# Decoder layers on one core: in the last attention, the queries' maxima reach all partitions by two DMAs and are put in order by ScalarE, and the exponentials run six steps behind the scores

## The chip, the cores and the metric

The kernel runs on one core of a Trainium2 chip. The core has TensorE (PE in the profile; PEld is its weight load), VectorE (DVE), ScalarE (ACT), GpSimd (POOL) and SyncE (SP), which here only issues DMAs. The metric is device time of one execution in microseconds, the median of several runs. Before the change it was 2773.41 us (three runs, 2769.01 to 2780.34).

## The reference

Four decoder layers of width 128 over a batch of 4 with 256 tokens each. Each layer has a self-attention, a cross-attention to a context of 1601 rows of width 96, and a feed-forward block, each followed by a residual and a layer norm. The change touches the last cross-attention only, which has 16 heads of 64:

```python
def _L3_xattn_ref(x, context, Wq, Wk, Wv, Wo, bo):
    HEADS, DIM_HEAD = 16, 64
    b, n, _ = x.shape                                   # 4, 256
    h, d = (HEADS, DIM_HEAD)
    scale = d ** (-0.5)
    q = (x @ Wq).reshape(b, n, h, d).transpose(0, 2, 1, 3)
    k = (context @ Wk).reshape(b, -1, h, d).transpose(0, 2, 1, 3)
    v = (context @ Wv).reshape(b, -1, h, d).transpose(0, 2, 1, 3)
    sim = jnp.einsum('bhid,bhjd->bhij', q, k) * scale
    attn = jax.nn.softmax(sim, axis=-1)
    out = jnp.einsum('bhij,bhjd->bhid', attn, v)
    out = out.transpose(0, 2, 1, 3).reshape(b, n, h * d)
    return out @ Wo + bo

x = _layernorm(x + _L3_xattn_ref(x, ctx_768, ...), axis=-1)
x = _layernorm(x + _L3_ffn_ref(x, ...), axis=-1)
```

The softmax subtracts, for each query and head, the maximum over all 1601 keys.

## The kernel before

All data is float32 but for a few masks and the last feed-forward. The program is a row of stages (`STAGES`, L2125); the last is `l3_xattn` (L1865). On PE, VectorE and ScalarE the order of its instructions is the order in which the code issues them (`manual_schedule`, L2060). Each engine works through its own list and stops at the first instruction whose input or buffer isn't ready. SP's list holds, in this stage, only the loads at its start and the four stores of the output.

A **unit** is one batch element and one pair of heads (L1875): 4 x 8 = 32 units. Head h of the pair lies in partitions 64h to 64h + 63 of the Q and K tiles. A unit has four **steps**: the keys in three groups of 512 and one of 65 (`parts`, L1888, splits a step into tiles of up to two chunks of 128 keys). I call a step of 512 keys full and one of 65 short. The loop at L2061 makes one pass for each step g, and in a pass does, for several steps at once:

- `queries` (L1894), once in a unit: Q of both heads, evicted by VectorE.
- `projections(g + 1, gb)` (L1902): K of the next step and V of step gb = g - LAG, into one PSUM tile, both evicted by ScalarE (L1931).
- `scores(g)` (L1933): keys in partitions, queries along the row. ScalarE copies the PSUM tile to an SBUF tile `St` (L1943).
- `running(g - 1)` (L1945): VectorE takes the elementwise maximum of the `St` tiles, so that after four steps there is one tile of 128 partitions x 2 heads x 256 queries.
- `maxima` (L1959), once in a unit: PE transposes this tile by matmuls with the identity, and VectorE reduces over the 128 keys (L1969). The result `mq` holds, in partition t, the four maxima of query t (2 heads x 2 halves of the queries).
- `spread` (L1971), once in a unit, one pass later: PE multiplies each column of `mq`, broadcast to 64 columns, with the identity, so that the maxima of all queries stand as a row in every partition. ScalarE copies this from PSUM to `Mb` (L1981).
- `shifted(gb)` (L1983): VectorE subtracts `Mb` from the `St` tiles of step gb. `weights(gb)` (L1991): ScalarE takes the exponentials in place.
- `sums(gb - 1)` (L1996): PE multiplies the exponentials with V into an accumulator that lives over the unit's four steps, and with ones for the row sums. After the fourth step ScalarE copies the row sums to `rows` (L2026).
- `ended` (L2029), issued one pass later by `advance(later)` (L2075): PE adds up the row sums, VectorE takes the reciprocal (L2035) and the product (L2038). After a batch element's eight units the output projection follows, and one pass at a time its layer norm and the last feed-forward (`l3_ffn`, L2087). `later` begins with what two batch elements have left over from the stage before, a feed-forward with GELU (L1796) among it.

PSUM has three large tiles for scores and projections (`big`) and two banks for all the rest (`misc`, named `one` in the profile); the accumulator holds one of the two banks for most of a unit. The lag is five steps and there are 12 `St` tiles. `kept` (L1883) is a part of a weight slot that is free by then; the running maximum and the leftovers live in it. Nearly all matmuls are recorded under L399, the helper `mm`.

## Time and profile before

| | |
|---|---|
| median of three runs | 2773.41 us |
| the profiled execution | 2769.6 us |
| its span | 2767.8 us, granted clock 0.98 |
| PE busy | 2620.8 us, 95% |
| VectorE busy | 1747.2 us, 63% |
| ScalarE busy | 1526.2 us, 55% |
| chain that ended last | PE 88%, DVE 6%, ACT 3% |
| the last attention | about 1896 us to the end |

The profile is one execution. The span runs from its first to its last instruction; the time of the execution is 1.8 us longer. Busy times are per engine, and engines overlap. Of a group of instructions the profile gives the line, the engine, the operation, the tile written and the tiles read with their shapes, the count, the busy time and the mean in nanoseconds; after it stands the idle time just before these instructions and what ended it. The chain that ended last follows the work back from the last instruction, at each step to what released it; it is given as start, length, engine, tile, line and count. `issue` is time in which an engine waited for nothing that the profile shows.

### The profile page before, as it was taken

The page shows a single profiled execution, that of the slowest core. Times are in us where ns is not written, and L with a number is a line of the kernel's source. Part 1 is how long each engine was busy: PE and PEld are TensorE (multiplying, and loading weights), DVE is VectorE, ACT ScalarE, POOL GpSimd, SP SyncE. Part 2 cuts the span into 40 slices and gives each one's busy share as a digit, 9 for nine tenths or more (in the row PEclk, how much of TensorE's full clock was granted, in tenths as well). Part 3 has the DMA queues.
Part 4 walks back from the last instruction along what each step waited for, and adds up shares of the span by engine and source line. Part 5 has one row for each costly group of instructions (what it writes and reads, how often), then busy time and mean ns, then how long its engine had stood idle before and what let it go on. Part 6 is the DMA issues. An engine that isn't in the chain of part 4 may idle for free.

```text
span 2767.8 us, 63295 instructions
## 1 busy us (share of the span) xinstructions
PE 2620.8 (95%) x26619; PEld 1708.1 (62%) x26619; DVE 1747.2 (63%) x3802; ACT 1526.2 (55%) x2931; POOL 180.2 (7%) x199
## 2 busy tenths in 40 slices
PE   6999999988879999999899999999999999999997
PEld 4555555555555555555797777776566666666665
DVE  5666666465457665655355666666677677677675
ACT  2455555635534555555554555556666576576573
POOL 2000100120020000000001011111000000000000
PEclk8999999989999999999999999999999999999999
DMA  3000000000120000000002010000000000000000
GB/s 111 2 1 1 2 1 1 1 21 15 27 88 17 2 1 1 1 2 1 1 1 87 20 25 13 13 12 3 1 1 2 4 2 1 3 2 2 3 2 3
DMA packets 14684, 34.57 MB, mean 12 GB/s; under 512 B 4025, under 2 KB 7229, under 8 KB 13505
## 3 DMA queue, kind: packets, MB, share of 16 engines
q1 hardware_dynamic: 14400, 30.53, 4.0%
q8 instruction: 210, 3.44, 0.5%
q14 instruction: 74, 0.60, 0.1%
HBM read 23.67 MB, written 0.52 MB: 9 GB/s over the span
## 4 chain that ended last, share of the span: by engine, by line
PE 88%; DVE 6%; ACT 3%; issue 2%; POOL 1%; DMA 0%; POOLq 0%; ACTq 0%; DVEq 0%
PE one L399 63%; PE big L399 13%; PE acc L399 8%; DVE M L909 1%; PE one L835 1%; PE one L544 1%; PE one L472 1%; DVE St L1987 1%; PE one L1324 1%; DVE mpad L697 1%; ACT E L731 0%; DVE w L1953 0%; DVE rec L2035 0%; POOL rn L1257 0%; ACT w L1314 0%
## 5 line engine op out<-in xcount | busy, mean ns | idle before, releaser
L909 DVE TENSOR_REDUCE M<-one 128x1 f32<-128x458 f32 (+3 forms) x1024 | 528.2, 567 | 290.8 <-PE one L399 289.8
L932 ACT ACTIVATE E<-one 128x512 f32<-128x512 f32 (+1 forms) x896 | 457.7, 563 | 420.8 <-PE one L399 420.7
L399 PE MATMUL one<-Q,K 32*128 32x256 f32 (+1 forms) x3328 | 531.8, 402 | 1.5 <-DVE M L909 1.5
L399 PE MATMUL one<-K,Q 32*128 32x458 f32 (+3 forms) x2048 | 459.2, 541 | 1.6 <-DVE M L909 1.6
L399 PEld LDWEIGHTS one<-Q,K 32*128 32x128 f32 (+1 forms) x3328 | 310.6, 180 | 62.3 <-DVE M L909 35.5
L1943 ACT COPY St<-big 128x1024 f32<-128x1024 f32 (+1 forms) x224 | 204.3, 959 | 160.0 <-PE big L399 160.0
L399 PEld LDWEIGHTS one<-K,Q 32*128 32x128 f32 x2048 | 171.2, 185 | 143.8 <-issue 79.3
L1987 DVE TENSOR_TENSOR St<-St,Mb 128x1024 f32<-128x1024 f32 (+1 forms) x224 | 245.2, 1141 | 1.8 <-ACT Mb L1981 1.8
L399 PE MATMUL acc<-E,V 128*32 128x256 f32 (+1 forms) x3328 | 233.2, 387 | 7.1 <-ACT E L932 7.1
L1994 ACT ACTIVATE St<-St 128x1024 f32<-128x1024 f32 (+1 forms) x224 | 215.1, 1014 | 25.4 <-DVE St L1987 25.3
L731 ACT ACTIVATE E<-one 128x384 f32<-128x384 f32 (+1 forms) x352 | 154.3, 525 | 115.0 <-PE one L399 114.8
L399 PE MATMUL big<-Q,K 64*128 64x256 f32 (+1 forms) x1664 | 214.4, 393 | 0.0
L399 PE MATMUL one<-St,V 128*64 128x256 f32 (+1 forms) x1664 | 205.7, 384 | 0.4
L492 POOL TENSOR_TENSOR ln_r<-ln_ve,half 128x2 f32<-128x2 f32 x92 | 71.0, 772 | 2070.0 <-DVE ln_ve L490 2015.8
L1953 DVE TENSOR_TENSOR w<-w,St 128x1024 f32<-128x1024 f32 (+1 forms) x160 | 178.5, 1116 | 34.8 <-ACT St L1943 27.6
L399 PE MATMUL one<-xT,w 128*128 128x256 f32 (+1 forms) x664 | 170.9, 398 | 18.8 <-DVE Q L1127 8.3
L692 DVE TENSOR_REDUCE Ms<-one 128x3 f32<-128x384 f32 x256 | 130.1, 550 | 89.0 <-PE one L399 87.8
L399 PEld LDWEIGHTS big<-Q,K 64*128 64x128 f32 (+1 forms) x1664 | 147.7, 183 | 57.5 <-issue 40.2
L399 PEld LDWEIGHTS acc<-E,V 128*32 128x32 f32 (+1 forms) x3328 | 87.3, 109 | 125.0 <-issue 70.0
L399 PEld LDWEIGHTS one<-St,V 128*64 128x64 f32 (+1 forms) x1664 | 114.3, 137 | 63.4 <-issue 15.9
L399 PEld LDWEIGHTS big<-w,ctx 96*64 96x64 f32 x1664 | 96.8, 137 | 54.0 <-issue 53.9
L399 PEld LDWEIGHTS one<-xT,w 128*128 128x128 f32 (+1 forms) x664 | 97.1, 181 | 50.2 <-issue 15.6
(308 smaller groups left out, 3743.7 us busy)
## 6 DMA issues: line engine op xcount, KB each, us to landing
QK<-qk SPq DMA_DIRECT2D x256, 16.0 KB
w<-in_p SPq DMA_DIRECT2D x12, 274.0 KB
rows<-in_ctx_rows SPq DMA_DIRECT2D x4, 630.5 KB
ctx<-in_ctx SPq DMA_DIRECT2D x4, 600.4 KB
w<-in_down SPq DMA_DIRECT2D x1, 2112.0 KB
w<-in_up SPq DMA_DIRECT2D x1, 1632.0 KB
w<-in_gp SPq DMA_DIRECT2D x1, 1632.0 KB
w<-in_p SPq DMA_DIRECT2D x4, 384.0 KB
```

Source lines behind the costliest of these rows:

```text
L399: self.nc.tensor.matmul(out, lhsT, rhs, start=start, stop=stop)
L472: self.nc.tensor.transpose(ps[:, n * P : (n + 1) * P], x[:, n, :], self.ident)
L492: nc.gpsimd.tensor_tensor(rstd, ve, self.half[:, :NB], ALU.pow)
L544: self.nc.tensor.transpose(ps[:rows, n * P : (n + 1) * P], m4[:, n, :rows], self.ident)
L692: nc.vector.reduce_max(out=m[:, j, :], in_=ps[:, : 3 * P].rearrange("p (s c) -> p s c", c=P), axis=AX.X,)
L731: nc.scalar.activation(es[t, j], ps[:, :w], AF.Exp, scale=scale)
L909: nc.vector.reduce_max(out=ms[i][:, n, j, part : part + 1], in_=ps[:, at : at + hi - lo], axis=AX.X)
L932: nc.scalar.activation(e[:kp, :w], ps[:kp, :w], AF.Exp, scale=scale)
L1943: nc.scalar.copy(st[:kp, :, :nc_, :], ps[:kp, :, :nc_, :])
L1953: nc.vector.tensor_max(to, to, sts[u, k][:kp, :, :nc_, :])
L1987: nc.vector.tensor_sub(e, e, top[u][:kp].unsqueeze(2).broadcast_to([kp, 2, nc_, T]))
L1994: nc.scalar.activation(e, e, AF.Exp, scale=HD**-0.5)
```

## The change

Spread's matmuls and its copy are replaced. The result `mq` of a unit's maxima (128 partitions x 4) is stored by a DMA into a DRAM tile `mrow`, and a second DMA reads it back, one row of 512 values to every partition, into `home`. In this row the four maxima of a query stand side by side. `order` has ScalarE copy it to `ordered`, where the queries of one head and half are contiguous. `home` and `ordered` lie in 1024 columns that are added to the tiles of two weight packs (`SPARE`); the slots of those packs have room for these columns, since larger packs use them earlier.

The DMAs are issued in the pass of `maxima`, right behind it; `order` comes two passes later, just before the first `shifted` of the unit, with the lag now six. `shifted` moves from ahead of `queries` and `projections` to behind them. `running` moves in one of four passes from the end of the pass to its beginning. There are 14 `St` tiles, and they are laid out chunk first, then head.

```diff
+SPARE = {"p4": 1024, "p3_3": 1024}
...
+        self.dram_pool = pool("dram", 2, space=bass.MemoryType.DRAM)
...
-        t = self.tile(f"w{SLOT[name]}", [P, src.shape[1]], pool=self.wpool)
+        t = self.tile(f"w{SLOT[name]}", [P, src.shape[1] + SPARE.get(name, 0)], pool=self.wpool)
...
-        HD, LAG = 64, 5
+        HD, LAG = 64, 6
...
+        o = self.dram["p3_3"].shape[1]
+        ordered = self.packs["p3_3"][:, o : o + 1024].rearrange("p (i j t) -> p i j t", i=2, t=P)
+        home = self.packs["p4"][:, 3 * NH * HD :].rearrange("p (i c) -> p i c", i=2)
...
-                st = self.tile("St", [P, 2, 2, T], bufs=12)
+                st = self.tile("St", [P, 2, 2, T], bufs=14)
                 sts[u, k] = st
-                nc.scalar.copy(st[:kp, :, :nc_, :], ps[:kp, :, :nc_, :])
+                nc.scalar.copy(
+                    st[:kp, :nc_, :, :].rearrange("p c h t -> p h c t"), ps[:kp, :, :nc_, :]
+                )
...
         def spread(u):
-            ps, m = self.misc(), mx.pop(u)
-            for j in range(2 * NB):
-                for d in halves:
-                    self.mm(
-                        ps[d, j * P : (j + 1) * P],
-                        m[:, j : j + 1].broadcast_to([P, HD]), self.ident,
-                    )
-            top[u] = self.tile("Mb", [P, 2, T], bufs=2)
-            nc.scalar.copy(top[u].rearrange("p h t -> p (h t)"), ps)
+            row = self.tile("mrow", [P, 2 * NB], bufs=2, pool=self.dram_pool)
+            nc.sync.dma_start(row, mx.pop(u))
+            top[u] = home[:, u % 2]
+            nc.sync.dma_start(
+                top[u], row.rearrange("t j -> (t j)").unsqueeze(0).broadcast_to([P, 2 * T])
+            )
+
+        def order(u):
+            nc.scalar.copy(ordered[:, u % 2], top.pop(u).rearrange("p (t j) -> p j t", j=2 * NB))
 
         def shifted(g):
             u = g // 4
+            m = ordered[:, u % 2].unsqueeze(1)
             for k, nc_, kp in parts(g):
-                e = sts[u, k][:kp, :, :nc_, :]
-                nc.vector.tensor_sub(
-                    e, e, top[u][:kp].unsqueeze(2).broadcast_to([kp, 2, nc_, T])
-                )
+                e = sts[u, k][:kp, :nc_].rearrange("p c h (n t) -> p c (h n) t", n=NB)
+                nc.vector.tensor_sub(e, e, m[:kp].broadcast_to([kp, nc_, 2 * NB, P]))
...
                 gb = g - LAG
-                if g % 4 < 2 and 0 <= g - 1 < steps:
+                if g % 4 < 3 and 0 <= g - 1 < steps:
                     running(g - 1)
-                if g % 4 == 1 and 4 < g <= steps + 1:
-                    spread(g // 4 - 1)
-                if 0 <= gb < steps:
-                    shifted(gb)
                 if 0 <= g + 1 < steps and (g + 1) % 4 == 0:
                     queries((g + 1) // 4)
                 if g + 1 < steps or gb < steps:
                     projections(g + 1, gb)
+                if 0 <= gb < steps:
+                    if gb % 4 == 0:
+                        order(gb // 4)
+                    shifted(gb)
                 if 0 <= gb < steps:
                     weights(gb)
                 self.advance(later)
...
                 if g % 4 == 0 and 4 <= g <= steps:
                     maxima(g // 4 - 1)
-                if g % 4 > 1 and 0 <= g - 1 < steps:
+                    spread(g // 4 - 1)
+                if g % 4 == 3 and 0 <= g - 1 < steps:
                     running(g - 1)
```

Where the diff is left out, `running`, `weights` and `sums` index the `St` tiles in the new layout.

More of the change, by code (lines that the diff above doesn't have):

```diff
@@ L1948, in running @@
                 if k == 1:
-                    mx[u] = kept[:, :4].rearrange("p (h c) t -> p h c t", h=2)
+                    mx[u] = kept[:, :4].rearrange("p (c h) t -> p c h t", h=2)
                     nc.vector.tensor_max(mx[u], sts[u, 0], sts[u, 1])
                 elif k:
-                    to = mx[u][:kp, :, :nc_, :]
-                    nc.vector.tensor_max(to, to, sts[u, k][:kp, :, :nc_, :])
+                    to = mx[u][:kp, :nc_]
+                    nc.vector.tensor_max(to, to, sts[u, k][:kp, :nc_])
             if g % 4 == 3:
@@ L1956, in running @@
                 mx[u] = self.tile("mx", [P, 2, T], bufs=2)
-                nc.vector.tensor_max(mx[u], m[:, :, 0, :], m[:, :, 1, :])
+                nc.vector.tensor_max(mx[u], m[:, 0], m[:, 1])
         def maxima(u):
@@ L1971, in spread @@
         def spread(u):
-            ps, m = self.misc(), mx.pop(u)
-            for j in range(2 * NB):
-                for d in halves:
-                    self.mm(
-                        ps[d, j * P : (j + 1) * P],
-                        m[:, j : j + 1].broadcast_to([P, HD]), self.ident,
-                    )
-            top[u] = self.tile("Mb", [P, 2, T], bufs=2)
-            nc.scalar.copy(top[u].rearrange("p h t -> p (h t)"), ps)
+            row = self.tile("mrow", [P, 2 * NB], bufs=2, pool=self.dram_pool)
[6 more added lines that the diff above has]
+            nc.scalar.copy(ordered[:, u % 2], top.pop(u).rearrange("p (t j) -> p j t", j=2 * NB))
         def shifted(g):
             u = g // 4
+            m = ordered[:, u % 2].unsqueeze(1)
             for k, nc_, kp in parts(g):
-                e = sts[u, k][:kp, :, :nc_, :]
-                nc.vector.tensor_sub(
-                    e, e, top[u][:kp].unsqueeze(2).broadcast_to([kp, 2, nc_, T])
-                )
+                e = sts[u, k][:kp, :nc_].rearrange("p c h (n t) -> p c (h n) t", n=NB)
+                nc.vector.tensor_sub(e, e, m[:kp].broadcast_to([kp, nc_, 2 * NB, P]))
         def weights(g):
             for k, nc_, kp in parts(g):
-                e = sts[g // 4, k][:kp, :, :nc_, :]
+                e = sts[g // 4, k][:kp, :nc_]
                 nc.scalar.activation(e, e, AF.Exp, scale=HD**-0.5)
@@ L2007, in sums @@
                             self.mm(
-                                acc[d, :T], vs[g][:, i - g % 4 * 4, d], e[:, h, c, :],
+                                acc[d, :T], vs[g][:, i - g % 4 * 4, d], e[:, c, h, :],
                                 start=i == 0, stop=False,
@@ L2016, in sums @@
                         self.mm(
-                            acc[d, T:], self.w("c", "ones", kp)[:, :SW], e[:, h, c, :],
+                            acc[d, T:], self.w("c", "ones", kp)[:, :SW], e[:, c, h, :],
                             start=False, stop=False,
@@ L2021, in sums @@
                     for h, d in enumerate(halves):
-                        self.mm(acc[d, :T], vs[g][:kp, 0, d], e[:, h, 0, :], start=False)
+                        self.mm(acc[d, :T], vs[g][:kp, 0, d], e[:, 0, h, :], start=False)
             vs.pop(g)
```

## The prediction

> **What bounds the kernel now.** I read first the page's busy times:

> ```profile
> PE 2620.8 (95%) x26619; PEld 1708.1 (62%) x26619; DVE 1747.2 (63%) x3802; ACT 1526.2 (55%) x2931; POOL 180.2 (7%) x199
> ```

> The changed stage is the last third of the span (about 1896 to 2767 us). The busy times of one stretch of it, one unit in the middle (columns: PE, PEld, DVE, ACT and POOL busy, granted clock, DMA share, GB/s):

> ```profile
> 2283.10:2307.68 24.58, 24.58 (x266) 15.43 (x264) 17.93 (x19) 16.86 (x24) 0.00 (x0) 1.00 0.01 1
> ```

> PE has no gap in 24.58 us, VectorE 6.7 us of gaps, ScalarE 7.7. So a PE instruction removed here is worth its whole length until another engine makes PE wait. The chain that ended last, over the same unit:

> ```profile
> 2283.10 3.75 PE one L399 x48
> 2286.85 1.93 PE big L399 x16
> 2288.78 1.02 PE one L399 x16
> 2289.80 1.73 PE big L399 x20
> 2291.53 1.14 PE one L399 x8
> 2292.67 3.07 PE big L399 x36
> 2295.74 3.16 PE one L399 x36
> 2298.90 1.93 PE big L399 x16
> 2300.83 0.58 PE one L399 x4
> 2301.41 1.73 PE big L399 x20
> 2303.15 2.73 PE one L399 x32
> 2305.88 1.81 PE big L399 x12
> ```

> Read as code: 3.75 is a full `sums` (2.73) and `maxima` (1.02); 1.93 `scores`; the second 1.02 is `spread`; 1.73 a full K and a full V projection; 1.14 the short `sums`; 3.07 is scores, short K and full V (so 1.14 for these two); 3.16 is `ended` (0.44) and sums; 0.58 `queries`; 1.81 is short scores (0.6), full K (0.86), short V (0.35).

> The instructions that the change touches, in groups over six units:

> ```profile
> L1987 DVE TENSOR_TENSOR St<-St,Mb 128x1024 f32<-128x1024 f32 x36 | 41.9, 1218 | 0.0
> L1994 ACT ACTIVATE St<-St 128x1024 f32<-128x1024 f32 x36 | 36.6, 1080 | 0.0
> ...
> L399 PE MATMUL one<-c,mq 128*64 128x128 f32 x96 | 6.6, 279 | 0.0
> ...
> L1981 ACT COPY Mb<-one 128x512 f32<-128x512 f32 x6 | 3.5, 586 | 0.0
> ```

> For the DMAs, an earlier stage's timeline has a small transfer on an empty queue, and the end has a store to DRAM:

> ```profile
> 1498.32 8.06 SPq L1850 DMA_DIRECT2D QK<-qk  x12
> ...
> 1501.03 0.40 PEld L399 LDWEIGHTS one<-QK 32*128 32x128 f32 x4 [2.31 <-DMA QK<-qk]
> ...
> 2765.16 0.37 SPq L2122 DMA_DIRECT2D out<-x  x1
> ```

> So 2.71 us from issue to use, and at most 2.64 for the store (the span ends at 2767.8).

> **Removed.** Spread's 16 PE instructions, 1.02 us in each of 32 units, all on the path. Its ScalarE copy (0.59) goes too; ScalarE isn't the bound.

> **Added: two DMAs a unit on SP's queue.** SP issues nothing else in this stage but four output stores, which wait for their block; a store issued just ahead costs the pair its issue (0.37), inside the spare time below. First, 16 bytes from each partition to DRAM: nearest row the store, 2.6. Second, 2 KB to each of 128 partitions: 2.7 as in the row, plus its packets. The page gives 14400 packets and 4.0% of 16 engines' span, so 0.123 us each; 8 an engine make 1.0. It can't start before the first has landed: 2.6 + 3.6 = 6.2 us. Bounds: 4.3 (twice 2.17, the shortest, QK<-w from 555.95 to 558.12) and 12.1 (twice 6.05, the longest DMA piece in the chain, four issues one behind another). I take 6.2, as nothing else is on the queue. [...]

> What hides them: the wait sits in ScalarE's queue at `order`, in the second step after maxima. From the end of maxima's matmuls PE does scores 1.93, K and V 1.21, sums 2.73, scores 1.93, K and V 1.14: 8.94. Call that end t0. ScalarE's turn comes at t0 + 0.7 (two copies). The reduction ends 1.1 after its matmuls (0.691 by its row, L1969, and up to 0.4 behind the shift of the same step). The pair may take 8.94 + 0.7 - 1.1 = 8.5; 2.3 are spare. Behind a late `order` stand, on ScalarE, this step's exponentials, the row-sum copy and the score evictions; PE waits for them.

> **Added: ScalarE's order**, 512 elements read 16 bytes apart: nearest row the 0.586 copy it replaces (contiguous, from PSUM). Bounds 0.4 (the 256-element copies, 0.373) and 2.3 (four times 0.586, as the read spans four times the bytes; no row excludes it). I take 0.59. [...]

> **Moved: shift after order, inside the same step.** At the step of t0 VectorE first does two running maxima (1.22 each), from t0 - 0.8, when the first eviction is there, to t0 + 1.65. ScalarE's order, from 0.7 to 1.3, hides behind them. Then two shifts (to 2.87 and 4.05), exponentials at 1.03 to 1.08 behind them (to 5.12), rows' copy (0.37, overlapping a little): 5.4. PE reaches `ended`, which reads rows, at t0 + 1.14 + 1.93 + 0.58 + 1.73 = 5.38. Before, the rows were there at 2294.87 and PE came at 2295.57, 0.7 spare; now none. I allow 0.1 a unit, +3 us; bounds 0 and 0.3 (+10). Every other pair keeps its order with room: maxima's input is done 0.9 before PE asks. The query copy now stands ahead of the shift; PE's wait for it at the three batch ends (0.48 each) should go: -1.4.

> **Same length:** the score copies, maxima, shifts and exponentials in the new layout move the same elements in runs of 128 or more; 224 of each, so 0.05 us apiece either way would stay in the 6 us of gaps. If those were gone, 4 x 224 x 0.05 = 45 us.

> **One step more behind.** Head: one more step without sums, PE work only moved. The first `order` has a shorter budget (6.5 us less 0.8), so +1. The GELU chain at 1996.6 to 2001.8, where PE waited 4.2 us for ScalarE, now falls on a short step (exponential 0.63 for 2.02): -1.4. Tail: after the last maxima PE has one full sums and a short V more left (3.1), which earlier lay ahead. Chain: reduction 0.75, pair 6.2, order 0.6, shift 1.2, two exponentials 2.1, rows 0.4, ended 0.44, then 2.73 + 0.97 + 2.73 + 0.35 + 2.73 + 1.14: 22.3. Before, 2724.24 to 2743.5: 19.3. 22.3 - 3.1 - 19.3 = 0, with the last unit's spread already inside; each us more of the pair costs one more here.

> **Sum:** 31 x 1.02 = -31.6; +3; -1.4; +1; -1.4; 0: -30.4. The profiled execution (2769.6, span 2767.8) would become 2739. It lies 3.8 under the median of the runs, 2773.4, so the median becomes 2743.

> **Rivals.**
> *The pair is late (slower).* Beyond 8.5 us, ScalarE's order starts late; 0.35 more hides behind the running maxima; from 8.85 each us costs PE one us in each unit, 32 in all. At 9.8 us (4.9 each) the gain is gone; at 12.1, 32 x 3.25 - 30 = +74: 2847. For it: 128 sixteen-byte packets to DRAM and a load at once behind them, which no row shows. Against: three rows of 2.2 to 2.7.
> *Order is slow.* Above 0.95 us it delays the shifts. At twice the row: 0.2 x 32 = 7 lost, 2750; at 2.3: 1.4 x 32 = 44, 2787.
> *The wait moves to rows (part of the gain).* At 0.3 a unit: 2750. For it: the zero margin above.
> *The change doesn't do what it says.* The DMA lands in spare columns of the tile that holds Wq, Wk, Wv. If projections waited for it as for the whole tile, PE would stand some 5 us a unit: +130, 2900. Against: the QK row, where matmuls of one tile's first 32 partitions start while its other DMAs are still out.

> **How the numbers follow.** Near the forecast (2734 to 2749) 0.58; part of the gain, by rows or order (2749 to 2759) 0.18; gain eaten to within 0.5% (about 14 us, what a measurement can tell here) 0.08; pair late, slower 0.09; order slow, slower 0.03; whole-tile waits and the rest 0.04. Low end 2734: no 0.1 allowance, no head cost, and 5 for a better head; high end 2766: reaches into the third case, leaving about 0.17 above. Faster 0.77, same 0.08, slower 0.15.

> **What would show it.** Right: a unit of 23.6 us with PE full; no `one<-c,mq` matmuls; ScalarE's order some 0.6 us without a wait on a DMA of any length in the middle of the stage; exponentials starting later after K and V. Wrong: PE or PEld waiting for ScalarE rows (L2026's successor) or the shift in each unit; ScalarE waiting for a DMA before order; order's mean over 1 us; PE waiting for a DMA at the projections. The forecast fails if the pair takes 9 us or more, or order more than 1 us.

## The result, and the profile after

The changed kernel takes 2781.51 us (median of 20 runs, 2773.02 to 2794.39), the kernel before beside it 2773.55 us (20 runs, 2765.99 to 2782.38). The ratio is 1.0031, 95% interval 1.0021 to 1.0041: a little slower, where 2743 us, 1.1% faster, was forecast. The profiled execution of the changed kernel spans 2779.3 us.

TensorE's code is now recorded under L402, the score copies under L1950, the order under L1992, the shift under L1999, the exponentials under L2004, the copy of the row sums under L2036.

A clock for the stage that needs no interpretation is the start of each unit's reduction to `mq` (L1969 before, L1978 after). From the timelines:

| us | before | after | forecast |
|---|---|---|---|
| one unit in the middle | 24.59 | 24.18 | 23.67 |
| the two intervals from the second batch end (reduction 16 to 18) | 59.95 | 63.27 | 57.6 |
| head: reduction 0 to 5 | 140.0 | 142.6 | 131.9 |
| all 31 intervals | 809.4 | 811.9 | 775.9 |
| tail: reduction 31 to the end of the span | 43.5 | 48.5 | 46.5 |
| reduction 0 to the end | 853.0 | 860.3 | 822.4 |

The last column is the forecast's own terms: 0.92 off each unit (1.02 removed, 0.1 allowed), 0.47 off each batch end, +1 - 1.4 at the head, and 3.1 us of sums and projections moved from the head (the longer lag) to the tail, where the chain was to be 3.0 longer (22.3 against 19.3). The stage is 7.3 us longer, close to the 8.0 between the medians. Everything ahead of the stage runs the same instructions in the same order in both kernels, so what the two spans differ by ahead of reduction 0 (4.1 us) is mostly how these two executions fell: in the kernels below, reduction 0 starts anywhere from 1911.8 to 1928.5 us.

So TensorE lost its 16 instructions in a unit, and gained much less. The busy times of one unit in the middle of the changed kernel (columns as before: the length, then PE, PEld, DVE, ACT and POOL busy, granted clock, DMA share, GB/s):

```profile
2229.00:2253.17 24.17, 23.93 (x250) 14.58 (x248) 18.03 (x18) 17.69 (x25) 0.00 (x0) 1.00 0.04 12
```

PE, full before, has a gap. The chain that ended last shows what ended it, in the same unit:

```profile
2228.41 0.82 ACT St L1950
2229.23 0.09 issue
2229.32 1.02 ACT St L1950
...
2230.41 0.21 ACT K L1938
2230.63 0.49 ACT V L1938
2231.11 1.03 ACT w L1992
2232.15 0.02 issue
2232.17 2.37 DVE St L1999 x2
...
2234.67 0.86 issue
2235.53 0.36 ACT rows L2036
2235.89 0.04 issue
2235.94 3.38 PE one L402 x36
```

For 7.5 us in each unit the chain leaves TensorE: two score copies, K and V copies, order, both shifts, the exponentials (their last part shows as 0.86 of issue), the row sums' copy, and only then `ended`. Before, these pieces were all on PE. The groups over two units (line, engine, operation, shapes, count; busy time and mean ns of one; idle before it and what ended that) say which link has the unexpected length:

```profile
L1999 DVE TENSOR_TENSOR St<-St,w 128x1024 f32<-128x1024 f32 x12 | 14.1, 1220 | 0.3 <-ACT w L1992 0.3
L2004 ACT ACTIVATE St<-St 128x1024 f32<-128x1024 f32 x12 | 12.5, 1068 | 5.8 <-DVE St L1999 5.5
L1950 ACT COPY St<-big 128x1024 f32<-128x1024 f32 x12 | 11.6, 1016 | 3.1 <-PE big L402 2.9
L1992 ACT COPY w<-w 128x512 f32<-128x512 f32 x2 | 2.3, 1146 | 0.0
```

Shift, exponentials and score copies are as long as before; order is 1.146 us, not 0.586. The waits of the stage (engine, tile and line, what it waited for: us in total, times, longest):

```profile
ACT St L2004 <- DVE St L1999: 116.5, 91, 2.5
...
PEld one L402 <- ACT rows L2036: 20.1, 28, 4.9
...
PE one L402 <- ACT rows L2036: 13.2, 27, 4.7
...
DVE St L1999 <- ACT w L1992: 11.8, 32, 6.0
```

The matmuls of `ended` wait for the rows in nearly every unit. At a batch end another wait is worse. PE's timeline there, and the busy times of four stretches around it:

```profile
2181.78 0.65 PE L402 MATMUL one<-xT,w 128*64 128x256 f32 x4 [2.19 <-ACT q8T L2118]
```

```profile
2176.00:2179.40 3.40, 3.40 (x30) 2.01 (x26) 3.12 (x4) 2.03 (x5) 0.00 (x0) 1.00 0.01 2
2179.40:2182.20 2.80, 0.61 (x6) 0.34 (x6) 0.97 (x1) 2.72 (x5) 0.00 (x0) 1.00 0.00 0
2182.20:2185.60 3.40, 3.40 (x25) 1.97 (x20) 2.69 (x3) 1.62 (x2) 0.00 (x0) 0.55 0.00 0
2185.60:2189.00 3.40, 3.40 (x20) 1.78 (x20) 2.88 (x10) 2.97 (x4) 0.47 (x1) 0.50 0.00 0
```

The queries of the next unit need the `misc` bank that the feed-forward's transposed row occupies until ScalarE has cast it (`q8T`, L2118), the accumulator having the other bank. The cast stands on ScalarE behind order and behind the exponentials, whose shift waits for order. PE stands for 2.19 us, and then the granted clock is 0.5 for 6.8 us, all of it work: about 3.4 us more (an estimate, half of the 6.8). This is the first of three batch ends inside the stage. At the second the wait is 2.21 us and PE is at half clock for 3.4 us, at the third it is 2.21 us and there is no half clock; the last section takes this up.

At the end of the stage the last unit's DMA pair lies open. The chain, after:

```profile
2730.90 0.61 DVE mq L1978
2731.52 0.02 issue
2731.53 1.38 DMA mrow<-mq
...
2732.99 3.97 DMA w<-mrow
2736.96 0.02 issue
2736.98 1.10 ACT w L1992
2738.08 0.02 issue
2738.10 2.37 DVE St L1999 x2
```

The pair takes 5.5 us from the end of the reduction to order. PE waits 4.69 us for these rows, until 2741.86, and the clock is at half from 2738.9 to 2745.7, so 3.84 us of work fall into it.

### The profile page after: what moved, and what is told of

It reads as the page before. It is cut to its first block, busy times and chain, and to the rows that moved or that the text cites. A ratio compares the mean times of both kernels' runs of the same rounds, so it can differ in the third digit from the quotient of the medians.

```text
span 2779.3 us, 62450 instructions
## 1 busy us (share of the span) xinstructions
PE 2609.4 (94%) x26107; PEld 1688.6 (61%) x26107; DVE 1751.8 (63%) x3802; ACT 1552.3 (56%) x2931; POOL 174.5 (6%) x199
## 3 DMA queue, kind: packets, MB, share of 16 engines
q8 instruction: 206, 3.38, 0.5%
## 4 chain that ended last, share of the span: by engine, by line
PE 81%; DVE 9%; ACT 6%; issue 3%; POOL 1%; DMA 0%; ACTq 0%; SPq 0%; POOLq 0%; DVEq 0%
PE one L402 60%; PE big L402 9%; PE acc L402 8%; DVE St L1999 3%; ACT St L1950 2%; DVE M L912 1%; ACT w L1992 1%; PE one L838 1%; PE one L547 1%; PE one L475 1%; PE one L1327 1%; DVE mpad L700 1%; ACT V L1938 0%; ACT E L734 0%; POOL rn L1260 0%
## 5 line engine op out<-in xcount | busy, mean ns | idle before, releaser
L402 PE MATMUL one<-Q,K 32*128 32x256 f32 (+1 forms) x3328 | 533.6, 404 | 1.5 <-DVE M L912 1.5
L402 PE MATMUL one<-K,Q 32*128 32x458 f32 (+3 forms) x2048 | 460.6, 544 | 1.6 <-DVE M L912 1.6
L402 PEld LDWEIGHTS one<-Q,K 32*128 32x128 f32 (+1 forms) x3328 | 312.1, 181 | 61.9 <-DVE M L912 35.5
L2004 ACT ACTIVATE St<-St 128x1024 f32<-128x1024 f32 (+1 forms) x224 | 220.6, 1005 | 121.3 <-DVE St L1999 116.5
L402 PEld LDWEIGHTS one<-K,Q 32*128 32x128 f32 x2048 | 173.0, 188 | 142.9 <-issue 80.0
L1950 ACT COPY St<-big 128x1024 f32<-128x1024 f32 (+1 forms) x224 | 204.0, 956 | 99.4 <-PE big L402 97.6
L1999 DVE TENSOR_TENSOR St<-St,w 128x1024 f32<-128x1024 f32 (+1 forms) x224 | 247.6, 1142 | 11.8 <-ACT w L1992 11.8
L402 PE MATMUL acc<-E,V 128*32 128x256 f32 (+1 forms) x3328 | 234.1, 388 | 7.0 <-ACT E L935 7.0
L402 PE MATMUL big<-Q,K 64*128 64x256 f32 (+1 forms) x1664 | 214.7, 393 | 0.0
L402 PE MATMUL one<-St,V 128*64 128x256 f32 (+1 forms) x1664 | 208.5, 388 | 4.0 <-DVE w L2048 2.8
L495 POOL TENSOR_TENSOR ln_r<-ln_ve,half 128x2 f32<-128x2 f32 x92 | 64.6, 702 | 2082.3 <-DVE ln_ve L493 2028.0
L402 PE MATMUL one<-xT,w 128*128 128x256 f32 (+1 forms) x664 | 169.8, 397 | 25.5 <-DVE Q L1130 8.3
L402 PEld LDWEIGHTS big<-Q,K 64*128 64x128 f32 (+1 forms) x1664 | 148.1, 184 | 57.8 <-issue 21.2
L402 PEld LDWEIGHTS acc<-E,V 128*32 128x32 f32 (+1 forms) x3328 | 87.7, 110 | 125.3 <-issue 70.7
L402 PEld LDWEIGHTS one<-St,V 128*64 128x64 f32 (+1 forms) x1664 | 115.8, 139 | 68.9 <-issue 21.3
L402 PEld LDWEIGHTS big<-w,ctx 96*64 96x64 f32 x1664 | 98.0, 139 | 55.0 <-issue 54.8
L402 PEld LDWEIGHTS one<-xT,w 128*128 128x128 f32 (+1 forms) x664 | 96.4, 181 | 56.7 <-issue 14.6
```

The costliest lines, as they stand in the source:

```text
L402: self.nc.tensor.matmul(out, lhsT, rhs, start=start, stop=stop)
L495: nc.gpsimd.tensor_tensor(rstd, ve, self.half[:, :NB], ALU.pow)
L1950: nc.scalar.copy(st[:kp, :nc_, :, :].rearrange("p c h t -> p h c t"), ps[:kp, :, :nc_, :])
L1999: nc.vector.tensor_sub(e, e, m[:kp].broadcast_to([kp, nc_, 2 * NB, P]))
L2004: nc.scalar.activation(e, e, AF.Exp, scale=HD**-0.5)
```

## The experiments

The expectations name theories by letters. A: order is longer than its row. B: the shift's new place in the pass, behind order, queries and projections, is too late. C: the lag of six steps itself costs. D: at batch ends, two small PSUM banks and the clock. Times of the kernel before in the four groups of runs were 2774.8, 2772.6, 2774.7 and 2778.2 us; each ratio is against its own group.

| kernel | unit | two intervals | head | 31 intervals | tail | reduction 0 to end | ratio (95%) |
|---|---|---|---|---|---|---|---|
| before | 24.59 | 59.95 | 140.0 | 809.4 | 43.5 | 853.0 | 1 |
| lag of six in before | 24.59 | 60.65 | 141.6 | 810.3 | 44.3 | 854.5 | 1.0002 (0.9987 to 1.0017) |
| after | 24.18 | 63.27 | 142.6 | 811.9 | 48.5 | 860.3 | 1.0031 (1.0021 to 1.0041) |
| contiguous read | 23.92 | 61.78 | 140.4 | 802.2 | 47.9 | 850.1 | 0.9993 (0.9976 to 1.0010) |
| no order, shift in front | 23.71 | 59.14 | 139.7 | 789.0 | 47.3 | 836.3 | 0.9949 (0.9931 to 0.9966) |
| order in front, ScalarE | 27.31 | 64.58 | 152.6 | 890.6 | 48.4 | 939.0 | 1.0329 (1.0301 to 1.0358) |
| order in front, GpSimd | 24.00 | 60.20 | 144.6 | 806.5 | 49.6 | 856.1 | 1.0026 (1.0014 to 1.0038) |
| cast on VectorE | 24.18 | 61.30 | 144.4 | 808.9 | 48.6 | 857.4 | 1.0010 (0.9998 to 1.0023) |
| order in front, VectorE | 23.71 | 59.81 | 143.5 | 797.4 | 48.8 | 846.1 | 0.9979 (0.9966 to 0.9992) |
| and last unit by PE | 23.75 | 59.81 | 144.3 | 799.5 | 44.4 | 843.9 | 0.9973 (0.9962 to 0.9984) |
| and queries first | 23.72 | 59.56 | 140.3 | 789.4 | 44.5 | 833.9 | 0.9929 (0.9914 to 0.9943) |

The columns in the middle are from one profiled execution of each kernel; the head, where half clock covers 12.3 us of PE's work after, 8.8 before and 6.8 with the lag alone, is the least certain: the mean granted clock of the changed kernel's 20 executions lies between 0.969 and 0.977. (Unit is the mean from reduction 12 to 16.)

**The lag alone (`x4_lag6`).** The kernel before with one line and one buffer changed:

```diff
-        HD, LAG = 64, 5
+        HD, LAG = 64, 6
...
-                st = self.tile("St", [P, 2, 2, T], bufs=12)
+                st = self.tile("St", [P, 2, 2, T], bufs=13)
```

> The kernel before with the lag of six steps alone (13 score tiles; maxima still spread by PE, shift at the front). Theory C (the lag itself costs: it moves the leftover and batch-end steps onto passes where the second PSUM bank comes free late, and PE's clock is halved after the waits): unit 24.58 as before, but 4 us more at each batch end and 5 at the head, the whole about 2788 or more. Theory B: the exponentials are early, so no bank comes free late: the same as before within 4 us, 2770 to 2778.

2775.38 us, ratio 1.0002 (0.9987 to 1.0017), the unit as before to 0.01 us, as B expected. As the cause of the loss in the middle units theory C falls. But the two ends of the stage are not what the forecast made them: the head is 1.5 us longer, though it should hold 3.1 us less of TensorE's work. PE's waits there, of this kernel:

```profile
1936.91 1.09 PE L399 MATMUL one<-c,mq 128*64 128x128 f32 x16 [0.72 <-DVE mq L1969]
1953.69 3.22 PE L399 MATMUL one<-St,V 128*64 128x256 f32 x16 [2.48 <-DVE w L2038]
1964.65 1.09 PE L399 MATMUL one<-c,mx 128*64 128x128 f32 x16 [0.67 <-ACT oT L477]
1992.36 1.09 PE L399 MATMUL one<-c,mx 128*64 128x128 f32 x16 [1.75 <-ACT xnT L512]
2001.27 1.40 PE L399 MATMUL one<-xnT,w 128*128 128x256 f32 x4 [2.73 <-ACT w L1796]
2052.66 1.09 PE L399 MATMUL one<-c,mx 128*64 128x128 f32 x16 [1.55 <-ACT xT L477]
```

With one more before them (0.96) they are 10.9 us. In the kernel before, PE's waits over the same units are four: 0.97, 0.48, 4.22 (the GELU) and 0.48, 6.2 in all. The 4.7 more are the main part of the 4.6 that are missing, though the sum is not exact: half clock covers 6.8 us of PE's work in this head and 8.8 before, which gives about 1 us back. The leftovers of the stage before, projection, norm and feed-forward, hand on from PE to VectorE or ScalarE and back once in a pass. I read the waits so that the sums which the longer lag moved away had covered these turns; no run puts other work there, so this reading is argued and not shown.

**Order without its stride, by another store (`x1_contig`, `x2_noorder`, `x3_front`).** To spare ScalarE the read at 16-byte distance, these store `mq` column by column, so that the row in DRAM already has the order of the queries. The first keeps the order copy, now contiguous; the second leaves it out and the shift reads `home`; the third also puts the shift at the front of the pass.

```diff
-            row = self.tile("mrow", [P, 2 * NB], bufs=2, pool=self.dram_pool)
-            nc.sync.dma_start(row, mx.pop(u))
+            row = self.tile("mrow", [2 * NB, P], bufs=2, pool=self.dram_pool)
+            nc.sync.dma_start(row.rearrange("j t -> t j"), mx.pop(u))
```

> The changed kernel, but the first DMA writes the maxima to DRAM column by column (4 bytes apiece), so that the row that comes back is already in order and ScalarE's order copies 512 contiguous elements. Nothing else moves. Theory A (the length of order is the cause: it took 1.146 us where the copy before took 0.586): order falls to about 0.6, the wait of PE for the row sums goes, a unit goes from 24.18 to about 23.6 us, the whole to about 2762. Theory B (the place of the shift is the cause: it stands behind the K and V copies and behind two running maxima, which end 1.77 us after the projections whatever order does, where order ended at 1.9): only 0.1 to 0.2 us a unit come back, 24.0 to 24.1, the whole 2775 to 2779.

> As the run before, but without order: the shift reads the row where the DMA put it; the shift keeps its place behind the projections and the running maxima. Theory A: unit 23.6 or less, the whole 2760. Theory B: the shift still waits for the running maxima, unit 24.0 to 24.1 as in the run before; the whole 2772 to 2778, a little less than it, since ScalarE has 0.6 us more in each unit.

> As the run before (no order), and the shift goes back to the front of its pass, ahead of queries and projections, with the running maxima where they were before the change. Theory A: no different from the run before. Theory B: the exponentials start right behind the V copy, the row sums are copied 2 us before PE asks for them, a unit is 23.56 us; at the batch ends PE no longer waits 2.2 us for the bank that ScalarE's int8 copy frees, and keeps its full clock; 31 x 0.62 + 3 x 4.5 + 5 at the head come back: the whole about 2743, and at most 2755.

2956.2, 2917.6 and 3024.6 us, ratios 1.0650 (1.0629 to 1.0671), 1.0513 (1.0495 to 1.0531) and 1.0895 (1.0874 to 1.0917). All three expectations missed, since the store changed more than order did. The timeline of the third:

```profile
2237.41 0.37 SPq L1984 DMA_DIRECT2D mrow<-mq  x1
...
2247.22 0.32 SPq L1986 DMA_DIRECT2D w<-mrow  x1
2250.57 2.36 DVE L1995 TENSOR_TENSOR St<-St,w 128x1024 f32<-128x1024 f32 x2 [6.43 <-DMA w<-mrow]
```

In this unit the load can be issued only 9.8 us after the store, in the median of the 32 units 8.7 (7.8 to 9.8). With 16 bytes from each partition it was 1.5 us (2731.53 to 2732.99 in the changed kernel, and 1.5 in the median of its units). The same 2 KB in 512 pieces of 4 bytes cost some 7 us more. The pair now takes some 13.2 us, and the engine that needs it first waits in each unit: in the first kernel

```profile
ACT w L1992 <- DMA w<-mrow: 131.2, 31, 8.9
```

These runs don't tell A from B, but they show the forecast's slower rival at work: a pair that is far past its deadline is paid in every unit. By that rival's rule, 13.2 against a deadline of 8.85 costs 32 x 4.35 = 139 us, some 2882 us; the first kernel took 74 more than that, at a mean clock of 0.946. They also give order's length when it reads contiguously, 617 ns.

**Order's length (`z1_contig_read`).** The changed kernel, the copy's read made contiguous; the store stays as it was, so the maxima are not put in order and a query is shifted by another query's maximum.

```diff
-            nc.scalar.copy(ordered[:, u % 2], top.pop(u).rearrange("p (t j) -> p j t", j=2 * NB))
+            nc.scalar.copy(ordered[:, u % 2], top.pop(u).rearrange("p (j t) -> p j t", j=2 * NB))
```

> The changed kernel, with one edit: order reads its 512 elements one after the other instead of 16 bytes apart, so that maxima reach other queries than their own (the permutation is left out; all other work stands). The DMAs are those of the changed kernel, so the wait of the two runs with the 4-byte store is not in it. Theory A (length of order): order 0.62 us as in the run with the column store, unit 24.18 to about 23.6 us, the whole about 2762. Theory B (place of the shift): the shift then waits for the running maxima, unit 24.0 to 24.1, the whole 2775 to 2779.

2771.87 us, ratio 0.9993 (0.9976 to 1.0010). Order's mean is 632 ns, the unit falls from 24.18 to 23.92, between what A and B expected, and the stage falls by 10.2 us. The stride of this one read, some 0.5 us in a unit, is worth 8 to 10 us in all: 0.26 in each unit, and 1.5 at each of two batch ends (at the third, where half clock fell this time, the two intervals are 0.5 longer). So the stride is shown as a cause, and not as the whole: the unit is still above what no wait at all would give.

**Order and the shift's place (`z3_front_noorder`).** No order, again with the permutation left out; the shift at the front of the pass and the running maxima placed as before the change.

```diff
+                if 0 <= gb < steps:
+                    shifted(gb)
                 if 0 <= g + 1 < steps and (g + 1) % 4 == 0:
                     queries((g + 1) // 4)
                 if g + 1 < steps or gb < steps:
                     projections(g + 1, gb)
...
-                    if gb % 4 == 0:
-                        order(gb // 4)
-                    shifted(gb)
```

> The changed kernel without order (the shift reads the row as the DMA left it, so the permutation is left out here too), and with the shift at the front of its pass and the running maxima where they were before the change. Theory B: no wait for row sums, unit 23.56 us; at the batch ends ScalarE's int8 copy is early and PE doesn't wait for its bank; the whole 2743 to 2752. Theory A: the whole 2762, as for the run with the contiguous read.

2758.42 us, ratio 0.9949 (0.9931 to 0.9966), under A's 2762 and above B's 2743 to 2752; the unit is 23.71, where B expected 23.56. So of the 0.47 us between 24.18 and 23.71, the read's stride makes 0.26, and the rest of order together with the shift's late place 0.21. Earlier shifts do meet the DMA now, and it costs nothing, as rows are there 2.2 us before PE asks:

```profile
DVE St L1995 <- DMA w<-mrow: 45.0, 28, 5.0
```

**Order at the front, on three engines (`x6_orderfront`, `y2_pool_order`, `y5_dve_order`).** All three compute everything. Shift and running maxima stand as in the last kernel; order comes ahead of the shift, on ScalarE, on GpSimd (issued with the DMAs), and on VectorE:

```diff
             u = g // 4
+            if g % 4 == 0 and u in top:
+                nc.vector.tensor_copy(
+                    ordered[:, u % 2], top.pop(u).rearrange("p (t j) -> p j t", j=2 * NB)
+                )
             m = ordered[:, u % 2].unsqueeze(1)
```

> The changed kernel with order and shift at the front of the pass, ahead of queries and projections, and the running maxima where they were before the change; order still reads 16 bytes apart (1.146 us), all values right. Theory A: no gain, 2775 to 2785. Theory B: order ends 1.25 us after the projections instead of 1.9, and the shift doesn't wait for running maxima: row sums are copied at 4.95 where PE asks at 5.46, unit 23.56 us; at the batch ends the bank of the int8 copy is still some 1.5 us late: the whole 2750 to 2760.

> As the run before, but GpSimd, which is idle in this stage but for the norms' powers, does the copy into order, right behind the DMAs; the shift at the front of its pass. All values right. Theory B: if GpSimd takes no more than 1.5 us for it, the shift starts at the front of the pass as in the run without order: the whole 2745 to 2755. If GpSimd takes 3 us or more, VectorE waits for it by the excess, and it is no better than 2765. Theory A: ScalarE is free of order, so 2762 or less too; this run doesn't tell A from B, the three others do.

> The changed kernel with the permutation done by VectorE ahead of the shift of a unit's first step, the shift at the front of the pass and the running maxima where they were in the kernel before; all values are computed. Theories A and B (length of order on the path to the rows, and the shift's late place) together: the permutation now has the time between the DMA's landing and the shift, so the unit stays near the 23.71 us of the run that left it out, some 2760 us (2755 to 2767), TensorE doesn't wait for the rows. Rival: the strided copy is as long on VectorE as on ScalarE (1.1 us) and stands ahead of the copy of Q, which TensorE then awaits as it did when order stood at the front on ScalarE: unit at 24.2 or more, 2775 to 2790 us.

On ScalarE: 2862.76 us, ratio 1.0329 (1.0301 to 1.0358), a clear miss. PE's timeline has, unit after unit:

```profile
2254.43 3.37 PE L402 MATMUL one<-St,V 128*64 128x256 f32 x16 [2.68 <-DVE Q L1907]
2282.47 1.95 PE L402 MATMUL one<-St,V 128*64 128x256 f32 x16 [2.68 <-DVE Q L1907]
2309.08 1.55 PE L402 MATMUL one<-St,V 128*64 128x256 f32 x6 [2.68 <-DVE Q L1907]
```

The first and the third of these lines have lengths of half clock: 3.37 us for 16 matmuls and 1.55 for 6, where the kernel before took 3.46 us for 16 at a granted clock of 0.50 (from 2731.15); the second takes 1.95 for 16. The timeline of all engines just ahead of the first line shows why PE waits:

```profile
2245.85 1.13 ACT L1992 COPY w<-w 128x512 f32<-128x512 f32 x1
...
2247.01 2.36 DVE L1999 TENSOR_TENSOR St<-St,w 128x1024 f32<-128x1024 f32 x2 [5.08 <-ACT w L1992]
```

Order has no wait for the DMA here (4.4 us in two of the 32 units, none in the others). It stands on ScalarE behind the score copies of the pass before, which wait for PE's scores. VectorE's shift waits 5.08 us for it; two running maxima and the next pass's shift follow, and the copy of Q stands behind them (at 2253.96). The accumulator needs the bank that Q leaves.

On GpSimd: 2781.03 us, ratio 1.0026 (1.0014 to 1.0038), a miss too. The shift waits for order, and at the head and the batch ends PE waits for the copy of Q behind it:

```profile
DVE St L1998 <- POOL w L1989: 77.3, 29, 6.2
```

GpSimd needs 1104 ns for the copy, less than the 1.5 us that the expectation allowed, but the copy begins only when the pair has landed. On VectorE: 2770.16 us, ratio 0.9979 (0.9966 to 0.9992), 3 us above the expected range. The unit is 23.71, as expected. Against the run without order the head is 3.8 us longer and the 26 intervals behind it 4.6 together; PE meets the copy of Q at the head and behind the batch ends. The copy is short there (from the last kernel below, the same instruction):

```profile
L2003 DVE COPY w<-w 128x512 f32<-128x512 f32 x3 | 1.9, 628 | 4.0 <-DMA w<-mrow 4.0
```

**The cast at the batch end (`x5_q8dve`).** The changed kernel with one line of the feed-forward altered:

```diff
-        nc.scalar.copy(qT, ps[:, :T])
+        nc.vector.tensor_copy(qT, ps[:, :T])
```

> The changed kernel with one copy moved: the feed-forward's cast of the queries' row (qT, line 2118), which stands on ScalarE behind order, shift and exponentials, goes to VectorE. Theory D (at the end of every other batch the wait for this cast holds one of the two small PSUM banks, TensorE stands 2.2 us and then runs 6.8 us at half clock, some 4.5 us each): the wait and the half-clock spell at 2193.8 and its likes go, 3 x 4.5 us, some 2768 us (2764 to 2772), while the steady unit stays at 24.2. Rival: VectorE has the running maxima and the shift in the same place, so the cast comes no earlier and the same wait and spell stand there: 2780 us (2777 to 2784).

2777.38 us, ratio 1.0010 (0.9998 to 1.0023): between theory and rival, about a third of what D expected. (The stage has three such batch ends inside it.) PE still waits at the place, but for less:

```profile
2186.81 0.65 PE L402 MATMUL one<-xT,w 128*64 128x256 f32 x4 [1.19 <-DVE q8T L2118]
```

```profile
2183.20:2186.60 3.40, 2.42 (x20) 1.50 (x18) 3.22 (x4) 2.03 (x3) 0.00 (x0) 1.00 0.01 2
2186.60:2190.00 3.40, 3.19 (x30) 1.74 (x30) 2.65 (x4) 3.40 (x6) 0.00 (x0) 1.00 0.00 0
```

A wait of 1.19 us instead of 2.19, and no half clock behind it at this end or the other two. The two intervals fall from 63.2, 63.3 and 62.3 to 61.3 at each end, 5 us together; before the change they were 59.95. So the cast's place does matter, with 1 to 2 us at an end, which is a third of what the ends lost against the forecast. Most of it is the half clock, which covered 10.2 us of work at the three ends of the changed kernel's execution and none here.

**The last unit (`y6_last_pe`).** The kernel with order on VectorE; the last unit's maxima alone are spread by matmuls, as before the change.

```diff
         def spread(u):
+            if u == len(units) - 1:
+                ps, m = self.misc(), mx.pop(u)
+                for j in range(2 * NB):
+                    for d in halves:
+                        self.mm(
+                            ps[d, j * P : (j + 1) * P],
+                            m[:, j : j + 1].broadcast_to([P, HD]), self.ident,
+                        )
+                nc.scalar.copy(ordered[:, u % 2].rearrange("p j t -> p (j t)"), ps)
+                return
```

> The run before (permutation on VectorE, shift at the front), and the last unit's maxima spread by eight matmuls and one ScalarE copy as in the kernel before, since no further work covers its DMA pair. If the tail's extra 4 to 5 us are the pair in the open: the stretch from the last reduction to the end falls from about 48 to about 44 us and the time lies 3 to 4 us under that of y5 (some 2756 if y5 gives 2760). Rival (the tail is bound by the shifts and exponentials of the last six steps instead): the same time as y5 within 1.5 us.

2765.90 us, ratio 0.9973 (0.9962 to 0.9984). The tail falls from 48.8 to 44.4 us, by what was expected; the ratios of the two kernels overlap, so the gain rests on the traces.

**Queries first (`y7_q_first`).** One more edit: Q's matmuls and copy ahead of order and shift, as the changed kernel has them.

```diff
+                if 0 <= g + 1 < steps and (g + 1) % 4 == 0:
+                    queries((g + 1) // 4)
                 if 0 <= gb < steps:
                     shifted(gb)
                 if g == steps + 1:
                     spread(len(units) - 1)
-                if 0 <= g + 1 < steps and (g + 1) % 4 == 0:
-                    queries((g + 1) // 4)
```

> The run before (permutation on VectorE, shift at the front, last unit spread by TensorE) with one edit: the queries and VectorE's copy of them come ahead of the permutation and the shift in a pass, as they do in the changed kernel. If what is left at the batch ends and at the head is TensorE waiting for the copy of Q behind the shift (11.4 us over 15 waits in the run before, 0.85 us in the open at a batch end): the wait goes, the second interval after a batch end falls from 27.1 to about 26.3 us, some 2760 us (2756 to 2765). Rival: the shift, now behind the copy of Q and so behind TensorE's queries, brings the exponentials and rows late again, and the unit goes from 23.71 to 23.9 or more: 2767 to 2775 us.

2756.44 us, ratio 0.9929 (0.9914 to 0.9943): faster than the kernel before by 0.7%, with every value computed. Between reductions 5 and 31 PE has no wait for Q left on its list, where the last kernel had 10.0 us of weight loads behind it in 13 waits. The second interval at a batch end falls only from 27.10 to 26.86 us, less than expected; at the second batch end the next two fall more, from 24.52 and 23.89 to 23.35 and 22.99. So the time is inside the expected range, but the interval that was to bring it is not what brought it. The unit stays, with PE full:

```profile
2245.00:2268.71 23.71, 23.71 (x252) 14.57 (x248) 18.66 (x20) 16.67 (x24) 0.00 (x0) 1.00 0.06 13
```

## Why the prediction was wrong, point by point

The mechanism of the gain was right: the DMAs are hidden and PE loses 16 instructions a unit. What failed is the count of PE's new waits. The step that put the wait at rows at 0.1 us a unit failed in every unit (0.47), together with order's length; the step "every other pair keeps its order with room" failed at the batch ends (15.9 us), and "PE work only moved" at the head (10.7 us). Two of the prediction's own signs of being wrong showed: PE waits for the rows in nearly every unit, and order takes over 1 us.

- **Where the gain was (removed: 16 PE instructions, 1.02 us in each unit).** Nearly right. With no wait in the way the unit is 23.71 us and PE is full, 0.88 less than 24.59. The chain's pieces of `big` matmuls add up to 12.34 us in such a unit against 12.20 before; why is not known. As a forecast of the whole, 31 x 0.88 = 27 instead of 31.6.
- **The pair (6.2 us, hidden).** Right: 5.5 us where the tail shows it, 5.8 in the kernel with order on VectorE (2715.36 to 2721.20), and in the changed kernel's list order waited for the DMA once only, in the last unit. The deadline of 8.85 us was not tested closely: with the 16-byte store the pair landed 5.0 to 6.5 us after the reduction wherever an engine waited for it, and in the three kernels that paid in every unit about 13.
- **Order (0.586 us taken, bounds 0.4 to 2.3).** Mis-sized: 1.146 us. The nearest row was contiguous, and the stride was the difference that mattered; read contiguously the copy takes 0.62 to 0.63. The rival "order is slow" tried twice the row, 1.17, which is nearly what ScalarE showed; it was a guess of mine, as no row of before has such a read. The price at that value (some 7 us) was near, against 8 to 10 measured. But it was booked as a rival, and it did not come alone.
- **The zero margin at rows (0.1 us a unit allowed, bounds 0 and 0.3).** This step failed in every unit. Its working was close: from t0, the end of the short projections at 2230.24, the running maxima end at 1.77 (1.65 worked out), order at 1.90 (1.3), the shifts at 4.29 (4.05), exponentials at 5.38 (5.12), rows at 5.64 (5.4). A quarter of a microsecond later than worked out, with a margin of nothing, made PE wait 0.24 us and its weight load 0.48; against the unit without waits it cost 0.47. I had counted the wait of one matmul, not the slower matmuls behind it: the 36 matmuls behind the wait take 3.38 us in the chain, where the same 36 took 3.16 before. And I gave a chain of seven pieces on two engines an allowance of 0.1, when half of its pieces had just been moved.
- **"Every other pair keeps its order with room", and Q at the batch ends (-1.4).** Wrong. PE's wait for the copy of Q did go, there is none in the changed kernel, but larger ones came. The two intervals there became 3.3, 3.3 and 2.4 us longer, not 2.3 shorter. Pairs within the attention were checked; the feed-forward's work that is interleaved there was not. Its cast stands behind order on ScalarE and holds one of two banks. Moving the cast gave back 5 us over the three ends, and the waits it left are 1.19 us for the cast and 0.78 for `y`. Another 0.7 of each end is the lag's, which moves work into these two intervals from the next (60.65 and 23.52 with the lag alone, 59.95 and 24.59 before).
- **Head (+1 and -1.4, "PE work only moved").** Wrong by 10.7 us: 142.6 against 131.9. The work was moved, but by the reading above it had been the cover of the leftovers' turns; with the lag alone PE's waits grow by 4.7 us. In the changed kernel PE's waits there are 13.3 us against 6.2, among them 2.77 for `w` (L2048), 2.59 for `xnT` (L515) and 3.19 for `w` (L1799, the GELU: 1.0 less than before, 1.4 was worked out), and half clock covers 12.3 us of PE's work instead of 8.8, which is some 1.7 us more. The best kernel's head is no shorter than before either, 140.3 us. Another spacing of the leftovers was not tried.
- **Tail (3.0 more in the chain, 3.1 less of work ahead).** Off by 2.0: 48.5 against 46.5. The chain from the reduction to the rows was worked out as 11.25 us and took 11.04. What was missed is the clock: the chain was worked out at full clock, and behind the 4.69 us of waiting 3.84 us of its work ran at half, which is 1.9 us. The kernel before could have shown it: behind a wait of 1.54 us its tail, the 19.3 of the sum, runs at half clock for 3.4 us (from 2730.9). That the tail could be covered was missed too: with one unit spread by matmuls it is 44.4.
- **Lengths in the new layout, and the lag.** Right: 1016, 1220 and 1068 ns, against 1023, 1219 and 1081; the lag alone 1.0002.

Put together: 30.4 forecast and 7.3 lost on the stage make 38 us. By the tables 10.7 lie at the head, 15.9 at the three batch ends (188.8 us for the six intervals against 172.9), 2.0 at the tail, and the remaining 9.4 in the 20 other units, nearly all of it the rows. The split is a rough one, since the lag moves work between intervals. Order's stride is inside these with 8 to 10. Counted over PE alone, from reduction 0 to the end, the change added 22.8 us of waits (45.7 against 22.9) and some 7 us by half clock (27.5 us of work at half clock against 13.3), and took away 22.5 us of work at full clock where 32 x 1.02 = 32.6 were forecast. Of the 10 that are missing there, some 6 are the slower matmuls behind a wait for rows (27 x 0.22) and some 4 the longer pieces of `big` (31 x 0.14), both estimates. The waits are of 0.2 to 5 us each, for neighbours that were "off the path" as long as spread or the sums stood in the way.

## What to carry to other kernels

When work is taken from a full engine, write down for every handover in the stage, the interleaved strangers' too, how long the data lies ready before that engine asks; the work removed is a gain only as far as these margins reach, and a margin of zero costs the wait and the slower matmuls behind it (0.24 and 0.22 us here). A copy with a stride is priced by a row with that stride on that engine, or tried on another engine (1146 ns on ScalarE here, 628 on VectorE). A DMA that is hidden by the next unit's work is bare in the last unit: there the old way may stay (the tail fell from 48.8 to 44.4 us here).

## What the runs showed of the hardware

- The same read of 512 floats at 16-byte distance takes ScalarE 1146 ns and VectorE 628; contiguous, ScalarE takes 617 to 632. GpSimd takes 1104 for the strided one. So the stride costs ScalarE some 0.5 us in this read. Whether it costs VectorE or GpSimd anything is open: no run has the contiguous copy on them. VectorE takes 294 ns for 256 contiguous floats from SBUF in another operation (L2111 of the changed kernel); twice that is 588, an estimate, against its 628.
- 2 KB from 128 partitions to DRAM: 1.5 us in the median from issue to the next DMA's issue in pieces of 16 bytes (the changed kernel), 8.7 in pieces of 4 (`x3_front`).
- Half clock for 6.8 us followed waits of PE's of 2.19, 2.77 and 2.59 us in the changed kernel, and not one of 3.19 at 2010.17; with order in front on ScalarE it followed, by the lengths of the matmuls, one wait of 2.68 us and not the next of the same length. So the length of a wait doesn't settle it. In the traces of the eleven kernels without the 4-byte store, every half-clock spell of the stage begins a whole number of 3.41 us after the first, so I cut the time into windows of 3.41 us and take those at full clock and PE's busy share in each. With a share of up to 0.44 all 54 were followed by half clock, with one over 0.62 none, between these 12 of 55. In the kernel before the three with shares of 0.00, 0.17 and 0.55 were followed by it; in the changed kernel the six of 0.00, 0.35, 0.36, 0.37, 0.45 and 0.49 were, and the five from 0.50 to 0.57 were not. The windows at the three batch ends of the changed kernel (columns as above):

```profile
2179.12:2182.53 3.41, 1.22 (x12) 0.55 (x10) 1.31 (x3) 3.18 (x5) 0.00 (x0) 1.00 0.00 0
2387.33:2390.74 3.41, 1.20 (x12) 0.58 (x10) 1.31 (x3) 3.13 (x5) 0.00 (x0) 1.00 0.00 0
2595.54:2598.95 3.41, 1.75 (x16) 1.03 (x18) 1.31 (x3) 3.33 (x6) 0.00 (x0) 1.00 0.02 5
```
